# A convolution-attention and mixture-of-experts kernel: the conditions of the rare expert tiles moved behind the other conditional tiles, and filler matmuls changed in two places

## The chip, the cores and the metric

The kernel runs on one core of one Trainium2 chip. The metric is the device time of one execution in microseconds (us). A core has five engines that this text calls PE (TensorE, the matmul array), DVE (VectorE), ACT (ScalarE), POOL (GpSimd) and SP (SyncE, which only issues DMAs); each runs its own instruction stream in order, and they meet through semaphores. "PEld" is PE's weight load, "PEq" or "PEldq" is PE's sequencer, the part that fetches, branches and hands work to the array. PE's clock is granted by a throttle; the profile shows it as a share of full speed.

## The reference, cut to what matters

The input is an image of 256 channels and 48 x 48 positions, that is 2304 tokens.

```python
x = x + _L0_conv_ref(_gn(x), ...)   # layer 0: group norm, then attention over 9216 = 2304 * 4 keys
t = _to_tokens(x)
t = t + _L1_attn_ref(_ln_t(t), ...) # layer 1: attention over 64 slices
t = t + _L1_ffn_ref(_ln_t(t), ...)  # layer 1: 8 experts, each token goes to its best 2
```

The expert part is what most of the change is about:

```python
top_w, top_i = jax.lax.top_k(xf @ Wg + bg, 2)
w_dense = sum over the 2 of one_hot(top_i) * softmax(top_w)
for e in range(8):
    h = gelu(xf @ W1[e] + b1[e])                  # 256 -> 1024
    out += w_dense[:, e:e+1] * (h @ W2[e] + b2[e])  # 1024 -> 256
```

## The kernel before, in words

**Start.** `x` is loaded in five pieces and each weight matrix by its own DMA. PE begins with `busy_first(14)` (L271): 14 matmuls whose result nobody reads, which I call fillers. They write columns 256 to 511 of the PSUM tile `pgb` (L263). PE then transposes `Wq` (L272), sums DVE's statistics over groups into columns 0 to 3 of the same `pgb` (L283), runs two more fillers (L297), and sums the variances (`spread`, L293 to L295). DVE and POOL make the normalisation from that (`rsqrt`, L301), DVE normalises `x` (L311), and the projections of q, k and v follow (L320, L324, L401), in PSUM tiles `pp` of a pool of five (L248).

**Attention of layer 0.** 18 blocks of queries by 36 pairs of key blocks; PE makes scores `s`, ACT takes their exponential `p`, DVE sums, PE multiplies with the values into `av`. Layer 1's attention is spread beside it and finished in a short stage of small steps.

**Routing.** The gate's results are turned into a list of 128-row tiles, each of one expert: 2 * 2304 = 4608 rows fill at least 36 tiles (`SURE`, L38) and, rounded up for each expert, at most 43 (`NSL`, L37). How many are used, `used_i`, is known only at run time; this input uses 39. Row numbers (`slot_t`) and experts (`expert_i`) of all tiles come out of matmuls `pw`, which are followed by four small matmuls `pq` and by `busy(8, spin)` (L1202), 8 more fillers. Every matmul here is float32 and appears in the trace as two records, so 8 fillers are 16 records.

**Expert tiles.** For tile `s`, POOL gathers 128 token rows with an indirect DMA (`rows`, L1246, or four parts, `parts`, L1257), SP loads the expert's `W1` (`load_w1`, L1271), PE (`turn`, L1278) or DVE (`turn_parts`, L1287) transposes the rows into `xT`, `first` (L1297) makes 16 matmuls `ph` and 8 gelus on ACT, `second` (L1315) 8 matmuls `py` and the scaling on DVE, and `scatter` (L1335) adds the rows to DRAM with an indirect DMA of POOL. `xT`, `hid`, `ph`, `py` and `y` are taken from small rings of buffers. Which expert a tile has is read from `expert_i` into a register on each engine.

The tiles come in three kinds, and their order in the program is written out by hand:

- `FAR` to `NSL - 1`, tiles 39 to 42, the rare ones. They stand first (L1355 to L1360), as four nested conditions `used > s`; ahead of them every engine reads `used_i` into a register (L1350).
- `near`, tiles 36 to 38. Tile 36 has no condition (L1382 to L1385). Tiles 37 and 38 stand in two nested conditions (L1386 to L1391).
- tiles 0 to 35, which always run (L1395 on).

With 39 tiles in use, all conditions of tiles 37 and 38 hold, and `used > 39` fails: every engine jumps over the code of all four rare tiles at once. In that place an engine also makes up for the semaphore counts of what it skipped: the instruction EVENT_SEMAPHORE at the condition's line, which waits for the count so far and then adds; on POOL also one INC_SWDGE_SEM, after waits for earlier indirect DMAs.

The last tile's rows are added in the output stage, and a second copy of the whole program, for inputs that overflow the exponential, is skipped by a condition at the very end (L1479).

Of the kernel before, what the change touches and what calls it, by code (L numbers as in the profile page):

```python
# [9 lines left out]
FP = mybir.dt.float32  # L10
# [5 lines left out]
P = 128  # L16
# [20 lines left out]
NSL = (2 * NT - E) // P + E  # L37
SURE = 2 * NT // P  # L38
FAR = SURE + 3
# [26 lines left out]
def layers(  # L66
# [10 lines left out]
    nc = tc.nc  # L77
# [7 lines left out]
    ones = const.tile([P, P], FP, name="ones")  # L85
# [72 lines left out]
    for c, pieces in enumerate(((1152, 1152), (1152, 768, 384))):  # L158
        at = 0
# [50 lines left out]
    for h in range(H1):  # L210
        at = ((h // 2) % 2 * 2 + h // 4) * D1
# [36 lines left out]
    with proj, tc.tile_pool(name="ps_pj", bufs=5, space=PSUM) as ps_pj, tc.tile_pool(  # L248
        name="ps_g", bufs=1, space=PSUM
    ) as ps_g, tc.tile_pool(  # L250
        name="ps_w", bufs=2, space=PSUM
    ) as ps_w:
        def transposed(dst, raw):
            pw = ps_w.tile([P, 2, C], FP, name="pw", tag="pw")
            for ci in range(2):
                for co in range(2):
                    pe.transpose(
                        pw[:, ci, co * P : (co + 1) * P], raw[:, co, ci * P : (ci + 1) * P], ident
                    )
            nc.scalar.copy(dst, pw)  # L260
            return dst

        pgb = ps_g.tile([P, 512], FP, name="pgb")  # L263

        def busy_first(n):
            for _ in range(n):
                pe.matmul(
                    pgb[:, 256:512], ones, ones.unsqueeze(1).to_broadcast([P, 2, P]), start=True, stop=True
                )

        busy_first(14)  # L271
        WqT = transposed(pj.tile([P, 2, C], FP, name="WqT"), raws["Wq"])  # L272
        pg = pgb[:, 0:4].rearrange("p (a b) -> p a b", a=2)
        pb = pgb[:, 16:94]
# [33 lines left out]
        for bi, (t0, tn) in enumerate(TBLOCKS):  # L308
# [6 lines left out]
            for m in range(2):  # L315
# [11 lines left out]
                for j in range(2):  # L327
                    rows = slice(j * DK, (j + 1) * DK)
                    at = (2 * m + j) * NT + t0
# [68 lines left out]
        for i in range(NTT):  # L398
            pv = ps_pj.tile([P, 512], FP, name="pp", tag="pp")
            for c in range(2):  # L400
                nc.tensor.matmul(  # L401
                    pv[:, 0:C], xn[:, c, i * P : (i + 1) * P], WvT[:, c, :],
                    start=(c == 0), stop=(c == 1),
# [15 lines left out]
    def busy(n, bank):  # L419

        for _ in range(n):
            pe.matmul(bank[:, 0:256], ident, Wqkv_sb[:, 0, 0:256], start=True, stop=True)
# [146 lines left out]
    def attention():  # L569
# [210 lines left out]
    spin = idle.enter_context(tc.tile_pool(name="ps_spin", bufs=1, space=PSUM)).tile(  # L780
        [P, 256], FP, name="spin"
    )
# [27 lines left out]
    for c in range(2):  # L810
        pe.matmul(
            pts[:, c, :], sums_of[:, c * P : (c + 1) * P], fold.rearrange("p a s -> p (a s)"),
            start=(c == 0), stop=False,
# [9 lines left out]
    for c in range(2):  # L823
        for i in range(NTT - 2, NTT):
# [3 lines left out]
                start=False, stop=(c == 1 and i == NTT - 1),  # L828
# [22 lines left out]
    with tc.tile_pool(name="sa", bufs=1) as sa, sums_done, tc.tile_pool(  # L851
        name="ps_sc", bufs=1, space=PSUM
# [9 lines left out]
        with tc.tile_pool(name="ps_b", bufs=3, space=PSUM) as ps_b:  # L862
# [5 lines left out]
            for m in range(2):  # L868
                for c in range(2):
                    pe.matmul(  # L870
                        ph[:, m, :], W0_sb[:, c, m * P : (m + 1) * P], ts_sum[:, c * S : (c + 2) * S],
                        start=(c == 0), stop=(c == 1),
# [28 lines left out]
            for u in range(2):  # L901
                ph = ps_b.tile([P, 2, 2 * S], FP, name="ph", tag="mm")
                phs.append(ph)
                for kind in range(2):
                    j = 2 * kind + u
                    for c in range(2):
# [3 lines left out]
                            start=(c == 0), stop=(c == 1),  # L910
# [5 lines left out]
            for u in range(2):  # L916
                for r in range(4):
                    v, w = divmod(r, 2)
                    rows = slice(r * D1, (r + 1) * D1)
# [14 lines left out]
            a = sa.tile([P, 2, 2, S], FP, name="a")  # L934
# [42 lines left out]
            for w in range(2):  # L977
                pe.matmul(
                    pw, tokT[:, w].rearrange("p a s -> p (a s)"), Wout_sb[:, w, :],
                    start=(w == 0), stop=(w == 1),  # L980
# [19 lines left out]
        with tc.tile_pool(name="ps_y0", bufs=1, space=PSUM) as ps_y0:  # L1000
# [3 lines left out]
            for g, (i0, n) in enumerate(groups):  # L1004
                pys = [next(banks)[:, 0 : C + E] for _ in range(n)]
                for i in range(i0, i0 + n, 4):
                    some = range(i, min(i + 4, i0 + n))
                    for k in some:
                        u = k % 2
                        rows = slice(u * S, (u + 1) * S)  # L1010
                        pe.matmul(
                            pys[k - i0], swT[rows, k // 2, :], tw[rows, :], start=(k >= 4),
                            stop=(k < 4 or k in by_dve),
# [29 lines left out]
    used_i = route.tile([1, 1], mybir.dt.int32, name="used_i")  # L1043
# [6 lines left out]
    with gating, tc.tile_pool(name="onehot", bufs=1) as oh, tc.tile_pool(  # L1050
        name="ps_lg", bufs=1, space=PSUM
# [112 lines left out]
        for n in (3, 6, 6, 3, 6, 6, 3, 3):  # L1164
# [13 lines left out]
            for j in range(k, k + n):  # L1178
# [3 lines left out]
                    start=(j == 0), stop=(j == K - 1),  # L1182
# [16 lines left out]
                pq[:, k, :], quad[:, k, :, :].rearrange("p q s -> p (q s)"), empties, start=True, stop=True,  # L1199
            )  # L1200
        dve.tensor_scalar(part_t, pq, 4.0, quarter, ALU.mult, ALU.add)
        busy(8, spin)  # L1202

    def expert_of(s, engine):
        return nc.values_load(
# [5 lines left out]
    with tc.tile_pool(name="ps_h", bufs=1, space=PSUM) as ps_h, tc.tile_pool(  # L1211
        name="ps_y", bufs=1, space=PSUM
    ) as ps_y, tc.tile_pool(name="ps_t", bufs=1, space=PSUM) as ps_t, tc.tile_pool(
        name="ps_j", bufs=1, space=PSUM
    ) as ps_j:

        def ring(pool, n, shape, name):
            return cycle([pool.tile(shape, FP, name=f"{name}{k}") for k in range(n)])

        ring_xs, ring_w1 = ring(fp, 2, [P, C], "xs"), ring(fp, 2, [P, 2, HID], "w1")  # L1220
        ring_xT, ring_hid = ring(fp, 3, [P, 2, P], "xT"), ring(fp, 2, [P, NHC, P], "hid")
# [4 lines left out]
        near_xs = iter([fp.tile([P, C], FP, name=f"near_xs{s}") for s in range(SURE, FAR)])  # L1226
        fin = ctx.enter_context(tc.tile_pool(name="fin", bufs=1))
        far_xs, far_w1 = fin.tile([P, C], FP, name="far_xs"), fin.tile([P, 2, HID], FP, name="far_w1")
        here = fin.tile([P, NT], FP, name="here")
        held = fin.tile([P, NTT], FP, name="held")  # L1230
        obs = cycle([fin.tile([P, 2, 512], FP, name=f"ob{k}") for k in range(3)])

        issued = []

        def indirect(**kwargs):

            new = nc.gpsimd.indirect_dma_start(**kwargs)  # L1237
            if issued:
                tc.add_manual_dep(
                    new.ins, issued[-1].ins.name,  # L1240
                    mybir.DependencyInfo(mybir.DependencyClass.NoSync, mybir.DependencyReason.DATA),
                    reason="in written order",
                )
            issued.append(new)

        def rows(s, xs):  # L1246
            indirect(
                out=xs, out_offset=None, in_=tn_d[:, :],
                in_offset=bass.IndirectOffsetOnAxis(ap=slot_t[:, s : s + 1], axis=0),
                bounds_check=NT + P - 1, oob_is_err=True,  # L1250
            )
            return xs

        def in_parts(s):
            return 2 <= s < SURE and s % 4 != 1
# [15 lines left out]
        def load_w1(s, w1):  # L1271
            e = expert_of(s, mybir.EngineType.SP)
            nc.sync.dma_start(
                out=w1, in_=W1[bass.ds(e, 1)].rearrange("e (p c) f -> p (e c) f", p=P)
            )
            return w1

        def turn(xs):  # L1278

            pt = next(ring_pt)  # L1280
            for c in range(2):
                pe.transpose(pt[:, c, :], xs.rearrange("p (d c) -> p c d", c=2)[:, c], ident)
            xT = next(ring_xT)
            dve.tensor_copy(xT, pt)
            return xT

# [10 lines left out]
        def first(s, xT, w1):  # L1297

            e = expert_of(s, mybir.EngineType.Activation)
            hid = next(ring_hid)  # L1300
            for f0 in range(0, NHC, 4):
                ph = next(ring_ph)
                for f in range(f0, f0 + 4):
                    for c in range(2):
                        pe.matmul(
                            ph[:, f - f0, :], w1[:, c, f * P : (f + 1) * P], xT[:, c, :],
                            start=(c == 0), stop=(c == 1),
                        )
                for f in range(f0, f0 + 4):
                    act.activation(  # L1310
                        hid[:, f, :], ph[:, f - f0, :], AF.Gelu, bias=b1_e[:, bass.ds(e, 1), f],
                    )
            return hid

        def second(s, hid, meanwhile):  # L1315

            e = expert_of(s, mybir.EngineType.PE)
            py = next(ring_py)
            for f in range(NHC):
                pe.matmul(  # L1320
                    py, hid[:, f, :],
                    w2_sb[:, bass.ds(e, 1), f, :].rearrange("p e d -> p (e d)"),
                    start=(f == 0), stop=(f == NHC - 1),
                )
                if f == 2:
                    meanwhile()
            e = expert_of(s, mybir.EngineType.DVE)
            y = next(ring_y)
            dve.tensor_tensor(
                y, py, b2_e[:, bass.ds(e, 1), :].rearrange("p e d -> p (e d)"), ALU.add  # L1330
            )
            dve.tensor_scalar(y, y, slot_w[:, s : s + 1], None, ALU.mult)
            return y

        def scatter(s, y):  # L1335

            indirect(
                out=t_d[:, :], out_offset=bass.IndirectOffsetOnAxis(ap=slot_t[:, s : s + 1], axis=0),
                in_=y, in_offset=None, bounds_check=NT + P - 1, oob_is_err=True,
                compute_op=ALU.add,  # L1340
            )

        near = range(SURE, FAR)
        xs, w1, xT, hid = {}, {}, {}, {}
        for s in near:
            xs[s] = rows(s, next(near_xs))
        for s in range(2):
            w1[SURE + s] = load_w1(SURE + s, next(ring_w1))
            xs[s] = parts(s, next(ring_xs))
        used = nc.values_load(  # L1350
            used_i, min_val=0, max_val=NSL,
            skip_runtime_bounds_check_because="it is a sum of counts, cut at NSL",
        )

        with ExitStack() as more:  # L1355
            for s in range(FAR, NSL):
                more.enter_context(tc.If(used > s))
                issued.clear()
                far = turn(rows(s, far_xs))
                scatter(s, second(s, first(s, far, load_w1(s, far_w1)), lambda: None))  # L1360
        issued.clear()

        def turn_next(s):
            if s in xs:
                xT[s] = (turn_parts if in_parts(s) else turn)(xs.pop(s))
# [17 lines left out]
        hid[SURE] = first(SURE, xT.pop(SURE), w1.pop(SURE))  # L1383
        w1[SURE + 2] = load_w1(SURE + 2, next(ring_w1))
        scatter(SURE, second(SURE, hid.pop(SURE), more_turns))  # L1385
        with ExitStack() as more:  # L1386
            for s in near[1:]:
                more.enter_context(tc.If(used > s))
                issued.clear()
                hid[s] = first(s, xT.pop(s), w1.pop(s))  # L1390
                scatter(s, second(s, hid.pop(s), lambda: turn_next(s + 1) if s + 1 in near else None))  # L1391
        issued.clear()
        for s in range(2):
            w1[s] = load_w1(s, next(ring_w1))
# [121 lines left out]
```

## Time and profile before

| what | value |
|---|---|
| median of 4 runs | 1603.0 us (1596.97, 1600.52, 1605.49, 1609.12) |
| the profiled execution | 1598.84 us |
| its span, first to last instruction | 1597.1 us |
| mean granted PE clock | 0.997 |
| PE busy | 1566.4 us (98%) |
| DVE, ACT, POOL busy | 1037.6 (65%), 830.2 (52%), 270.5 us (17%) |
| matmuls `s` and `av` of layer 0's attention, busy | 674.8 and 675.7 us |
| matmuls `ph` and `py` of the experts, busy | 150.8 and 144.4 us |

The profile is of one execution. Its times count from the span's start. "Idle before" is the time for which an engine did nothing ahead of an instruction, and the name behind it is what released it; "issue" is time in which the engine waited for nothing that the profile shows. A PE record's duration overlaps the next one's, so sums of durations are no times; starts are compared instead.

### The profile page before, as it was taken

Reading aid. Unit: us, or ns where it says so; the run is one execution under the profiler, and the core shown is the slowest. Engines: PE = TensorE matmul, PEld = TensorE weight load, DVE = VectorE, ACT = ScalarE, POOL = GpSimd, SP = SyncE. Lnnn points to the kernel's source line nnn. Section 1 sums busy time; section 2 is a strip of 40 time slices with the busy share of each in tenths; the row PEclk is TensorE's granted clock in tenths of the full one; section 3 lists DMA queues with packets and bytes.
Section 4 is the critical chain, followed back from the end, with each engine's and each line's share of the span. In section 5 each row is a group of like instructions: output and inputs, shape, how many; then the busy total and the mean of one; then the engine's idle time right before and its main releaser. Section 6 shows DMA issues by size and latency. Waiting matters only on the chain. (4 is left out here: it accounts for less than half of the span.)

```text
span 1597.1 us, 32306 instructions
## 1 busy us (share of the span) xinstructions
PE 1566.4 (98%) x13105; PEld 781.7 (49%) x13105; DVE 1037.6 (65%) x1323; ACT 830.2 (52%) x1168; POOL 270.5 (17%) x210
## 2 busy tenths in 40 slices
PE   8999999999999999999999999999999999999998
PEld 5633343333333333333333333333335789898996
DVE  7578787787787877878878778778786711211111
ACT  2366665655665666556556556566554623322322
POOL 0001101011011010110100101101100146666571
PEclk9999999999999999999999999999999999999999
DMA  4000000000000000000000000000003846655665
GB/s 136 1 1 1 1 1 4 6 1 1 8 1 1 8 1 2 8 1 1 6 3 1 4 5 1 1 8 1 1 1 113 297 139 190 179 172 154 193 169 160
DMA packets 53071, 79.32 MB, mean 50 GB/s; under 512 B 22719, under 2 KB 43406, under 8 KB 47790
## 3 DMA queue, kind: packets, MB, share of 16 engines
q1 hardware_dynamic: 42834, 66.45, 12.6%
q0 software_dynamic: 9424, 10.10, 3.6%
q8 instruction: 108, 1.77, 0.5%
q10 hardware_dynamic: 652, 0.56, 0.1%
q14 instruction: 53, 0.43, 0.1%
HBM read 62.94 MB, written 12.32 MB: 47 GB/s over the span
## 5 line engine op out<-in xcount | busy, mean ns | idle before, releaser
L60 ACT ACTIVATE p<-s 128x1024 f32<-128x1024 f32 x648 | 663.3, 1024 | 470.4 <-PE s L60 465.8
L60 DVE TENSOR_TENSOR acc<-acc,p 128x1024 f32<-128x1024 f32 x612 | 749.5, 1225 | 243.2 <-ACT p L60 237.3
L60 PE MATMUL av<-p,v_sb 64*64 64x512 f32 x5184 | 675.7, 590 | 2.9 <-ACT p L60 1.8
L60 PE MATMUL s<-q,kk 64*64 64x512 f32 x5184 | 674.8, 589 | 0.5 <-DVE tn L60 0.5
L60 PEld LDWEIGHTS s<-q,kk 64*64 64x64 f32 x5184 | 202.1, 133 | 353.6 <-issue 181.5
L60 PEld LDWEIGHTS av<-p,v_sb 64*64 64x64 f32 x5184 | 195.6, 131 | 358.4 <-ACT p L60 201.5
L60 POOL PARTITION_ALL_REDUCE total<-both x17 | 71.2, 4187 | 1011.4 <-ACT p L60 833.5
L60 ACT ACTIVATE hid<-ph,bcol 128x128 f32<-128x128 f32 x312 | 88.8, 370 | 210.8 <-PE ph L60 118.8
L60 PE MATMUL ph<-xT,w 128*128 128x128 f32 x1248 | 150.8, 279 | 3.7 <-issue 3.3
L60 PEld LDWEIGHTS ph<-xT,w 128*128 128x128 f32 x1248 | 149.2, 195 | 7.1 <-issue 5.1
L60 PE MATMUL py<-w_sb,hid 128*128 x624 | 144.4, 380 | 2.9 <-issue 2.6
L60 PEld LDWEIGHTS py<-w_sb,hid 128*128 128x128 f32 x624 | 114.7, 190 | 18.3 <-issue 4.2
L1237 POOL DMA_INDIRECT xs<-tn_d,part_t x104 | 106.6, 1025 | 40.1 <-issue 29.3
L60 DVE TENSOR_TENSOR y<-py,b_bc 128x256 f32<-128x256 f32 x39 | 16.6, 425 | 127.1 <-PE py L60 83.4
L1237 POOL DMA_INDIRECT t_d<-y,slot_t x38 | 61.6, 1620 | 69.1 <-DVE y L60 35.6
L60 DVE STREAM_TRANSPOSE xT<-xs 128x128 f32<-128x128 f32 x52 | 13.1, 289 | 61.6 <-DMA xs<-tn_d,part_t 56.7
L60 DVE COPY xT<-pt 128x256 f32<-128x256 f32 x13 | 5.4, 424 | 54.0 <-PE pt L60 54.0
L60 DVE RECIPROCAL rinv<-rinv 128x256 f32<-128x256 f32 x17 | 29.7, 1746 | 0.0
L60 POOL TENSOR_TENSOR rstd_t<-ve,mhalf 128x2 f32<-128x2 f32 (+2 forms) x13 | 11.1, 851 | 103.4 <-DVE ve L60 96.1
L60 DVE TENSOR_TENSOR acc<-p 128x1024 f32<-128x1024 f32 x18 | 22.1, 1226 | 4.9 <-ACT p L60 3.3
L337 DVE TENSOR_SCALAR q<-pp,bcol 64x512 f32<-64x512 f32 (+1 forms) x30 | 20.8, 694 | 6.1 <-PE pp L320 5.8
L60 DVE TENSOR_REDUCE up<-av 128x512 f32<-128x1024 f32 x17 | 20.8, 1225 | 5.0 <-PE av L60 5.0
(302 smaller groups left out, 616.2 us busy)
## 6 DMA issues: line engine op xcount, KB each, us to landing
w<-in_L_ffn_W_dram SPq DMA_DIRECT2D x39, 1024.0 KB
w_sb<-in_L_ffn_W_dram SPq DMA_DIRECT2D x8, 1024.0 KB
t_sb<-turned SPq DMA_DIRECT2D x224, 8.0 KB
x_sb<-in_x_dram SPq DMA_DIRECT2D x3, 576.0 KB
xs<-tn_d,part_t POOLq DMA_INDIRECT x104
t_d<-t_sb SPq DMA_DIRECT2D x2, 768.0 KB
tn_d<-tn SPq DMA_DIRECT2D x2, 768.0 KB
t_sb<-t_d SPq DMA_DIRECT2D x3, 512.0 KB
```

The source lines that it names most:

```text
L60: return self.tc.keep_in_program_order(getattr(self.engine, name)(*args, **kwargs))
L337: nc.vector.tensor_scalar(dst, pq[rows, 0:tn], bcol[rows, B_Q + m : B_Q + m + 1], 0.125, ALU.add, ALU.mult,)
L1237: new = nc.gpsimd.indirect_dma_start(**kwargs)
```

## The change

It has four parts.

1. The fillers of the start write a PSUM tile of their own, `spun`, the first tile of the pool `pp`; `pgb` shrinks to 96 columns. The first row of fillers has 17 matmuls instead of 14. The pair of fillers at L297 stays, but in the new tile.
2. The fillers after `pq` are 6 instead of 8.
3. The read of `used_i` and the four conditions of the rare tiles move from ahead of tile 36: the read stands behind tile 36, and the rare tiles stand behind tile 38, inside the conditions of tiles 37 and 38.
4. The rare tiles take their transposed rows from a tile of their own, `far_xT`, not from the ring `xT`.

```diff
-        pgb = ps_g.tile([P, 512], FP, name="pgb")
+        pgb = ps_g.tile([P, 96], FP, name="pgb")
+        spun = ps_pj.tile([P, 512], FP, name="pp", tag="pp")
...
-                    pgb[:, 256:512], ones, ones.unsqueeze(1).to_broadcast([P, 2, P]), start=True, stop=True
+                    spun[:, 0:256], ones, ones.unsqueeze(1).to_broadcast([P, 2, P]), start=True, stop=True
...
-        busy_first(14)
+        busy_first(17)
...
-        busy(8, spin)
+        busy(6, spin)
...
+        far_xT = fin.tile([P, 2, P], FP, name="far_xT")
...
-        def turn(xs):
+        def turn(xs, xT=None):
...
-            xT = next(ring_xT)
+            xT = next(ring_xT) if xT is None else xT
...
-        used = nc.values_load(
-            used_i, min_val=0, max_val=NSL,
-            skip_runtime_bounds_check_because="it is a sum of counts, cut at NSL",
-        )
-
-        with ExitStack() as more:
-            for s in range(FAR, NSL):
-                more.enter_context(tc.If(used > s))
-                issued.clear()
-                far = turn(rows(s, far_xs))
-                scatter(s, second(s, first(s, far, load_w1(s, far_w1)), lambda: None))
-        issued.clear()
-
...
         scatter(SURE, second(SURE, hid.pop(SURE), more_turns))
+        used = nc.values_load(
+            used_i, min_val=0, max_val=NSL,
+            skip_runtime_bounds_check_because="it is a sum of counts, cut at NSL",
+        )
         with ExitStack() as more:
             for s in near[1:]:
                 more.enter_context(tc.If(used > s))
                 issued.clear()
                 hid[s] = first(s, xT.pop(s), w1.pop(s))
                 scatter(s, second(s, hid.pop(s), lambda: turn_next(s + 1) if s + 1 in near else None))
+            for s in range(FAR, NSL):
+                more.enter_context(tc.If(used > s))
+                issued.clear()
+                far = turn(rows(s, far_xs), far_xT)
+                scatter(s, second(s, first(s, far, load_w1(s, far_w1)), lambda: None))
         issued.clear()
```

In the built program PE's order around the change is: before, `pw`, `pq`, 8 fillers, read of `used_i`, jump over the rare tiles, tile 36, tile 37, tile 38, tile 0; after, `pw`, `pq`, 6 fillers, tile 36, read of `used_i`, tile 37, tile 38, jump over the rare tiles, tile 0. POOL's four part gathers for tile 2 stand ahead of tile 36's scatter in both; before, that is behind the jump, after, ahead of it. SP's load of `W1` for tile 38 stands behind the jump before and ahead of it after.

## The prediction

> **What bounds the kernel now.** I read the page first: span, busy times and clock.
>
> ```profile
> PE 1566.4 (98%) x13105; PEld 781.7 (49%) x13105; DVE 1037.6 (65%) x1323; ACT 830.2 (52%) x1168; POOL 270.5 (17%) x210
> ...
> PEclk9999999999999999999999999999999999999999
> ```
>
> PE is busy for 98% of the span at nearly full clock, and in the attention (about 45 to 1215 us) nearly without a gap. So whatever moves PE's start of the projections moves the end by as much, and so does a gap of PE among the expert tiles. The change touches three places; for each I read PE's timeline.
>
> At the start:
>
> ```profile
> 1.12 7.76 PE L60 MATMUL pgb<-ones 128*128 128x256 f32 x28 [1.12 <-DVE ones L86]
> 10.41 0.63 PE L60 MATMUL pw<-ident,Wq_raw 128*128 128x128 f32 x4 [1.53 <-DMA Wq_raw<-in_L_conv_Wq_dram]
> 11.06 0.35 PE L60 MATMUL pgb<-mv,gmat 128*128 128x2 f32 x2
> 12.12 1.13 PE L60 MATMUL pgb<-ones 128*128 128x256 f32 x4 [0.70 <-DVE mean L60]
> 13.09 0.28 PE L60 MATMUL pgb<-dm,gmat 128*128 128x2 f32 x2
> ```
>
> The second fillers (12.12) wait for DVE to have read `pgb`, only because they write the same tile; the sum over `dm`, which everything waits for, stands behind them.
>
> Between routing and experts:
>
> ```profile
> 1277.25 0.98 PE L60 MATMUL pq<-empties,quad 128*128 128x43 f32 x8
> 1278.06 3.70 PE L60 MATMUL spin<-Wqkv_sb,ident 128*128 128x256 f32 x16
> 1283.16 0.48 PE L60 MATMUL pt<-ident,near_xs 128*128 128x128 f32 x2 [1.39 <-PEq L1355]
> 1284.19 5.38 PE L60 MATMUL ph<-xT,w 128*128 128x128 f32 x32 [0.56 <-issue]
> ```
>
> PE waits 1.39 us for its own sequencer at L1355, the condition of the rare tiles. The instructions of that line, and those of the conditions of tiles 37 and 38:
>
> ```profile
> L1355 PEldq COMPARE_BRANCH x1: 4134/4134/4134, 1278.6 to 1278.6; - x1
> L1355 DVEq COMPARE_BRANCH x1: 72/72/72, 1279.0 to 1279.0; - x1
> ```
> ```profile
> L1386 PEldq COMPARE_BRANCH x3: 73/85/205, 1290.9 to 1306.2; - x3
> ```
>
> The jump over four tiles takes PE's sequencer 4.134 us, from 1278.6 to 1282.7; DVE's takes 72 ns, and a condition of PE that does not jump far 73 to 205 ns. The 16 filler records cover 3.2 us of the jump. Then the clock, in stretches of 3.41 us (columns: stretch, length, PE busy, PEld, DVE, ACT, POOL, granted clock, DMA):
>
> ```profile
> 7.51:10.92 3.41, 1.88 (x11) 1.28 (x9) 3.35 (x8) 0.00 (x0) 0.00 (x0) 1.00 0.74 238
> 10.92:14.33 3.41, 2.68 (x19) 2.21 (x17) 0.88 (x6) 0.94 (x2) 0.55 (x1) 1.00 0.81 226
> 1280.68:1284.09 3.41, 1.56 (x8) 0.92 (x6) 0.42 (x1) 0.00 (x0) 2.69 (x3) 1.00 0.42 118
> 1284.09:1287.50 3.41, 3.31 (x15) 3.34 (x16) 0.00 (x1) 0.00 (x0) 0.00 (x0) 0.50 0.14 41
> 1475.24:1478.65 3.41, 1.59 (x14) 1.49 (x13) 0.08 (x1) 0.27 (x2) 1.83 (x2) 1.00 0.12 29
> 1478.65:1482.06 3.41, 3.41 (x18) 3.41 (x18) 1.11 (x4) 1.97 (x8) 2.09 (x2) 0.50 0.79 267
> ```
>
> After a stretch in which PE was busy for 1.56 or 1.59 us the clock is halved for the next 3.41 us; after 1.88 us it is not. The price is in the timeline: tile 36's 32 `ph` records took 5.38 us, the other tiles' 3.73, so 1.65 us. The point lies at about 1.75 us busy, or 1.66 us idle.
>
> Last, where the jump goes, between tiles 38 and 0:
>
> ```profile
> 1304.78 3.62 PE L60 MATMUL py<-w_sb,hid 128*128 x16
> 1308.23 3.73 PE L60 MATMUL ph<-xT,w 128*128 128x128 f32 x32
> ```
>
> There is no gap here. The last L1386 instruction, the end of tile 38's code, is at 1306.2 on PE's sequencer: it runs 2.0 us ahead of the array's next start, 1308.23.
>
> **The change, step by step**, against the profiled execution (1598.84 us; its span is 1597.1, with 1.74 around it).
>
> *A. Fillers with a bank of their own.* The pair no longer waits for `mean`: it follows the sums at 11.06 + 0.35 = 11.41 instead of 12.12. `dm` is ready by about 12.0 (two DVE instructions of 0.35 us together from 11.65), earlier than the fillers' end. The sum over `dm` comes 13.09 - 12.12 = 0.97 after the pair's start, so at 12.38: 0.7 us sooner. Behind it every step waits for the one before (DVE `ve` 13.53, POOL 13.78, DVE `t_sb` 14.55, PE `pp` 15.15), and the transposes of `Wv`, done 0.78 us before `pp`, cover 0.7 even if their weight comes no sooner. **-0.7 us**; ends -0.7 and 0.
>
> *Three more fillers* are 6 records. 16 records in 3.70 us are 0.22 us each at full clock, so 1.3 us: 8.88 + 1.3 = 10.2, before `Wq` lands at 10.41. Idle time hides them: 0. Without that cover, at half clock, 2.6 us would end at 11.5 and delay the sums by up to 1.1. I take 0, ends 0 and +1.1.
>
> *B. Tile 36 without a jump ahead of it.* PE loses two fillers (4 records, 0.9 us) and the jump. The fillers then end at 1281.76 - 0.9 = 1280.9. Next is tile 36's gather, which POOL starts at 1277.33 (1.38 us long). The trace does not show when it landed, as PE was held by the jump. The nearest row is a later gather that DVE did wait for: start 1538.78, DVE's transpose at 1541.32, 2.54 us; with the 0.37 by which this one is longer, 1280.2. So the fillers decide, and `pt` starts at 1280.9 instead of 1283.16: **-2.25 us**; ends -2.25 and 0 (landing only just before 1283.1). PE's idle time falls from 1.39 + 0.56 to some 0.6, under 1.66, so the half clock goes too: **-1.65**; ends -1.65 and 0.
>
> *C. The jump behind tile 38.* It starts where PE's sequencer stands at 1306.2, takes 4.13 us, and 0.43 us pass from the jump's end (1282.7) to the first record, as at L1355: 1310.8 instead of 1308.23, **+2.55 us**. Nothing covers more than the 2.0 us of run-ahead counted. PE then stands idle for about 2.4 us, over 1.66; only if the edge of a stretch cuts the gap in the middle is the clock spared, in some 3 of 10 positions. **+1.65**; ends 0 and +1.65. The jump's ends: 0, if it is as short as the conditions of L1386 (0.2 us at most, under the run-ahead), and +2.55.
>
> The rest costs nothing. The read of `used_i` behind tile 36 (about half a us on a sequencer) lies under PE's run-ahead of over 2 us. On ACT, DVE and SP the jump takes under 0.1 us, in their idle time. On POOL, what stands behind the jump is the gather for tile 3; POOL must first see tile 38's scatter land (3.84 us from issue in the chain of waits: 1309.53 + 3.84 = 1313.4, and about 1 us of bookkeeping). That gather waits anyway until PE has transposed tile 1's rows, 1312.2 before, 2.55 us later now. They meet; if PE were not delayed, POOL would be late by about 2 us, and the 7 us from the gathers' landing (about 1316.55 + 2.54 = 1319.1) to PE's use (1326.1) would cover it. SP's loads are released by PE as before. `far_xT` never runs here; the ring order of the others keeps its distances.
>
> Sum: -0.7 - 2.25 - 1.65 + 2.55 + 1.65 = **-0.4 us**, so 1598.4 for this execution. The median of the four runs is 1603.0, 4.2 above the profiled one, which is among the fastest; on it the sum is **1602.6**. The jump is not saved, it is moved: from a place with 3.2 us of cover to one with 2.0.
>
> **Two rules.** The Trainium skill, "Advanced Engine Details and Errata" (Control Flow Timing), gives a compare-and-branch about 108 ns; by that C would be nearly free and the sum 1598.5. But "Runtime: NRT & Kernel Launch" (Instruction fetch mechanics) says that a taken branch to code outside the two loaded pages stops until it is fetched, and the 4134 ns agree with the latter.
>
> "TensorE: Matmul & The Clock Gate" (HAM oscillation) asks for no idle gap above about 3.4 us. By that C's gap would leave the clock alone, and the sum would be 1600.9; the row at 1280.68, with gaps of 1.39 and 0.56 only, speaks against it.
>
> **Rivals.** *R1, the jump is short or hidden behind tile 38.* For it: the 73 to 205 ns of L1386 and DVE's 72 ns. Against: the same distance cost PE 4.134 us. C falls away: 1603.0 - 0.7 - 2.25 - 1.65 = 1598.4.
>
> *R2, slower: tile 36 is held by its gather, not by the jump.* The place is PE at 1283: if the gather lands close to 1283, PE idles as before, with two fillers fewer and the half clock still there; B gives 0. Then 1603.0 - 0.7 + 2.55 + 1.65 = 1606.5. It decides from a landing later than about 1282.6, where the idle time passes 1.66. For it: POOL's first gather is longer than the rest (1.38 us against 1.01), and the chain of waits has indirect DMAs that took 3.84 us to land.
>
> *R3, the added fillers are late.* The first fillers took up to 795 ns each, the later ones 379; if that slow part lasts longer in a run, the 0.2 us of slack is gone: +1.1, 1603.7.
>
> *R4, the change of the bank does nothing* (the pair still waits): A is 0, 1603.3.
>
> **How the numbers follow.** Chances: forecast 0.45, R1 0.15, R2 0.22, R3 0.10, R4 0.08. The runs of the same kernel spread from 1597.0 to 1609.1, more than any of these cases differ from the forecast; about 0.5%, 8 us, is what a measurement can tell from no change. The range runs from R1 less 3 to R2 plus 3.5, half of the runs' spread being 6: **1595.5 to 1610**. Faster than 1595.0 has 0.12 (R1 with a favourable set of runs), slower than 1611.0 0.14 (R2 or R3 with an unfavourable one), within 0.74.
>
> **What the new profile would show.** A: the second fillers start right behind the sums, and `pp` near 14.5. B: `pt` of tile 36 under 0.3 us behind the last filler, and tile 36's 32 `ph` records in about 3.7 us. C: a COMPARE_BRANCH of some 4.1 us on PE's sequencer behind tile 38, a PE gap of 2 to 2.6 us ahead of tile 0, and tile 0's `ph` records at 5.4 us. I am wrong if that branch is short, if `pt` waits for the gather, or if PE has new gaps in the attention, where nothing is changed.

## The result, and the profile after

| | before | after |
|---|---|---|
| median | 1599.9 us (78 runs) | 1603.2 us (52 runs) |
| ratio to before, 95% interval | | 1.002 (1.0008 to 1.0032) |
| the profiled execution, its span | 1598.84, 1597.1 us | 1603.11, 1601.4 us |

The change costs 0.2%, some 3.3 us of the medians. That is under the half per cent named in the prediction, but it is on the other side of zero than the forecast, and its interval does not hold a ratio of 1. That the forecast time, 1602.6 us, comes so near to the measured 1603.2 is luck: it was reckoned from a median of four runs, 1603.0, where 78 runs have 1599.9; from that the forecast's -0.4 us would have given 1599.5.

PE's timeline of the changed kernel at the start (start, length, engine, line, operation, shapes; in brackets the idle time before and its releaser):

```profile
1.12 9.96 PE L60 MATMUL pp<-ones 128*128 128x256 f32 x34 [1.12 <-DVE ones L86]
10.92 0.63 PE L60 MATMUL pw<-ident,Wq_raw 128*128 128x128 f32 x4
...
12.57 0.28 PE L60 MATMUL pgb<-dm,gmat 128*128 128x2 f32 x2
13.44 0.26 PE L60 MATMUL pgb<-ident,brow 78*128 78x78 f32 x1 [0.59 <-DMA Wo_raw<-in_L_conv_Wo_dram]
...
15.35 0.70 PE L321 MATMUL pp<-t_sb,WqT 128*128 128x512 f32 x1 [0.78 <-DVE t_sb L312]
```

DVE's timeline of the same kernel shows who waits for the transpose of the biases (`brow`):

```profile
13.73 0.16 DVE L60 TENSOR_SCALAR ve<-pgb 128x2 f32<-128x2 f32 x1 [1.32 <-PE pgb L60]
13.81 0.23 DVE L60 COPY bcol<-pgb 128x78 f32<-128x78 f32 x1
```

The sum over `dm` comes 0.5 us sooner, yet `ve`, which needs only that sum, starts at 13.73. It reads `pgb`, and the transpose of `brow` writes another part of the same tile; that transpose waited until 13.44 for a load. (The view names the load of `Wo`; by the landings it was the last piece of the biases, in at 13.24, where before it was in at 12.31.) So `pp` starts at 15.35, 0.2 us later than before. The first fillers ended at 11.08 in this execution, later than `Wq` could have been taken. But the sums over `mv` at 11.41 follow DVE's `mv` (ready at 11.26) as closely as before (10.92 and 11.06), so the fillers are not seen to delay them.

Between routing and experts, and at the jump's new place, again PE's timeline of the changed kernel:

```profile
1277.64 2.84 PE L60 MATMUL spin<-Wqkv_sb,ident 128*128 128x256 f32 x12
1280.31 0.39 PE L60 MATMUL pt<-ident,near_xs 128*128 128x128 f32 x2
1281.22 3.84 PE L60 MATMUL ph<-xT,w 128*128 128x128 f32 x32 [0.52 <-DVE xT L60]
...
1300.23 3.62 PE L60 MATMUL py<-w_sb,hid 128*128 x16
1307.91 6.34 PE L60 MATMUL ph<-xT,w 128*128 128x128 f32 x32 [4.06 <-PEq L1379]
```

`pt` follows the fillers without a gap and tile 36 runs at full clock: this part of the gain is there. The price stands at 1307.91: 4.06 us idle and 6.34 us for tile 0's records. The instructions of the conditions' line (now L1379; min, median and max in ns):

```profile
L1379 SPq COMPARE_BRANCH  x4: 34/41/50, 1285.8 to 1286.9; - x4
L1379 PEldq COMPARE_BRANCH  x4: 65/142/5510, 1286.7 to 1307.6; - x4
L1379 DVEq COMPARE_BRANCH  x4: 43/51/67, 1289.9 to 1305.2; - x4
```

The long one is PE's jump, from 1301.69 to 1307.20: 5.510 us, where it took 4.134 before. And the clock by stretches (columns as in the prediction):

```profile
1303.00:1306.41 3.41, 0.85 (x4) 0.39 (x3) 0.78 (x2) 0.00 (x0) 1.44 (x1) 1.00 0.47 192
1306.41:1309.82 3.41, 1.91 (x9) 1.94 (x10) 0.00 (x0) 0.00 (x0) 0.13 (x1) 0.50 0.33 46
1309.82:1313.23 3.41, 3.41 (x18) 3.41 (x18) 0.00 (x0) 1.14 (x4) 0.00 (x0) 0.50 0.00 0
```

Two stretches at half clock follow the gap, not one.

What holds the jump up is in the records of single DMA packets. The profile has two "instruction" queues; the one called q8 moves code in packets of 16 KB. I take it for PE's, as in every run with a long branch of PE one of its packets starts and ends inside that branch. The packet for this jump started at 1304.79, 3.10 us after the branch; the load of `W1` for tile 1 (1 MB) moved from 1301.43 to 1305.03. Before the change the packet came 1.79 us after the branch, and no such load was moving.

### The profile page after: what moved, and what is told of

Same layout as the page of the kernel before. It is cut to its first block, busy times and chain, and to the rows that moved or that the text cites. A ratio compares the mean times of both kernels' runs of the same rounds, so it can differ in the third digit from the quotient of the medians.

```text
span 1601.4 us, 32303 instructions
## 1 busy us (share of the span) xinstructions
PE 1569.5 (98%) x13107; PEld 781.7 (49%) x13107; DVE 1037.0 (65%) x1323; ACT 829.2 (52%) x1168; POOL 270.0 (17%) x210
```

## The experiments

The theory, **J**: the move puts a jump that must fetch its code into a place with little cover, where a load delays the fetch, and the clock is halved after the gap. The rivals: **S**, the new start is what costs; **F**, the moved code disturbs what follows it, and not the jump itself. The experiments ran on chips where the kernel before takes 1583.9 us (the two parts alone, no rare code, side by side), 1584.1 us (one rare tile, both with fillers, no load) and 1584.6 us (the rest). I call the last one the third chip, and that of the profiles above the first. Times are medians, ratios are to the kernel before on the same chip.

### The two parts alone

*The start alone* (before, with part 1 of the change) and *the move alone* (after, with the old start and 8 fillers behind `pq`):

```diff
-                    pgb[:, 256:512], ones, ...
+                    spun[:, 0:256], ones, ...
-        busy_first(14)
+        busy_first(17)
```


> The kernel before with the first part of the change alone (fillers in a tile of their own, 17 instead of 14); the conditions and the 8 fillers stay as before. Theory J (the jump behind tile 38 lies bare and makes the loss): the time is that of before within 1 us, the first projection starts at 14.5 to 15.4 us, and tile 36 waits for PE's sequencer at L1355's place as before. Rival S (the fillers of the start make the loss): 2 to 3 us slower than before, with the projections later by as much.

> The changed kernel with the start of before and 8 fillers ahead of tile 36; the rare conditions stay behind tile 38. Theory J: a branch of 4 to 5.6 us on PE's sequencer behind tile 38, 7 to 7.7 us from the last py row of tile 38 to tile 0's first ph (3.45 before), tile 0's ph stage at 5.2 to 6.2 us (3.57 before); the time is that of the changed kernel plus 0 to 0.5, so 2 to 4 us over before. Rival S: the time of before, within 1 us.

Measured: the start alone 1582.22 us, 0.9991 (0.9982 to 1.0000); the move alone 1588.48 us, 1.0030 (1.0018 to 1.0042). So the start alone is some 1.4 us faster than before, a little more than J allowed. S falls, the move is the whole loss. F falls too: from tile 1 to the last `ph` it is 246.9 us in both, so nothing behind the jump is disturbed. The move's jump took 6.174 us, over the 4 to 5.6 expected, with a gap of 4.73 us behind tile 38. With the start alone, `pp` began at 14.31, since `brow` had landed and its transpose waited for nothing.

### Without the rare tiles' code

The changed kernel without the loop over the rare tiles. That code never runs for this input.

```diff
-            for s in range(FAR, NSL):
-                more.enter_context(tc.If(used > s))
-                ...
```


> The changed kernel with the code of the four rare tiles left out, which this input never runs. Theory J: no long branch, 3.5 us from the last py row of tile 38 to tile 0's first ph, tile 0's ph stage at 3.6 us, and the time is 6 to 7 us under the changed kernel, so 3 to 4 us under before. Rival S: at most 1 us under the changed kernel. Rival F (the moved code disturbs the loading of later instructions, which shows as 'issue' gaps among the tiles 0 to 35): the jump's gap goes, but the gaps after 1400 us stay and the gain is under 3 us.

Measured: 1579.72 us, 0.9975 (0.9966 to 0.9984). No branch of PE between tiles 36 and 0 takes more than 0.33 us, and `ph` of tile 0 follows `py` of tile 38 without a gap. Against the changed kernel itself (1.0020, below) code that is never run makes 0.45%, some 7 us.

### Side by side instead of nested; one rare tile instead of four

```diff
-                more.enter_context(tc.If(used > s))
-                issued.clear()
-                ...
+                with tc.If(used > s):
+                    issued.clear()
+                    ...
```


> The changed kernel with the four rare conditions side by side instead of nested, so that PE makes four jumps over one tile each. Theory J with the price set by the distance: four branches of 0.1 to 0.3 us and about 0.4 us of bookkeeping each, 2 us in all, covered by PE's run-ahead: no gap, 4 to 6 us under the changed kernel. If the price is set by the code that has to be loaded on the way, not by the distance of one jump: the branches add up to 4 us or more again, and the gap stays at 2 to 4 us.

Measured: 1588.46 us, 1.0034 (1.0021 to 1.0048), no gain. PE's branches of this kernel:

```profile
L1386 PEldq COMPARE_BRANCH x5: 176/214/3352, 1300.3 to 1307.6; - x5
```

Of four short jumps, those at 1300.31 and 1302.79 took 0.24 and 0.21 us, the one at 1303.36 took 3.352, the next 0.21. The price does not belong to a branch that is taken, nor to each tile; it falls once. PE's gap is 5.54 us even so, more than the 2 to 4 expected: the second branch comes only behind the end of `py` at 1302.45, so no work of PE is left to cover the long one.

```diff
-            for s in range(FAR, NSL):
+            for s in range(FAR, FAR + 1):
```


> The changed kernel with the code of one rare tile instead of four (tiles 40 to 42 are left out, which this input never runs), so PE's jump is a quarter as long. Theory J with the price set by the distance: a branch of 0.1 to 0.3 us and no gap, as without rare tiles. If any jump out of the straight line costs the same: 4 to 5.6 us and the gap of the changed kernel.

Measured, with the code of tiles 40 to 42 left out, which this input does not run: 1583.22 us, 0.9991 (0.9981 to 1.0002). The jump over one tile's code took 0.24 us, PE's gap was 0.68 us, and the clock stayed whole there. The Trainium skill, "Runtime: NRT & Kernel Launch" (Instruction fetch mechanics), says that a taken branch whose target lies outside the two pages loaded forces a fetch before execution can go on; these two runs, with one long branch of 3.352 us beside short ones of about 0.2, and the code packets below agree with it.

### Fillers ahead of the jump

```diff
+            busy(10, next(ring_py))
+            next(ring_py)
             for s in range(FAR, NSL):
```


> The changed kernel with 10 fillers (20 records, 4.4 us) between tile 38 and the rare conditions. Theory J, in two terms: the branch stays at 4 to 5.6 us but PE has work meanwhile, so no gap over 1 us, no half clock and tile 0's ph stage at 3.6 us instead of 6.2; the fillers cost 4.4 us where the gap was 4.1, so the time is 2 to 2.6 us under the changed kernel. If the half clock had no part in the loss: within 0.5 us of the changed kernel.

Measured: 1588.49 us, 1.0030 (1.0019 to 1.0042): no gain, against the expectation. PE's timeline of this kernel:

```profile
1302.39 4.48 PE L60 MATMUL py<-Wqkv_sb,ident 128*128 128x256 f32 x20
1307.57 0.35 PE L60 MATMUL ph<-xT,w 128*128 128x128 f32 x1 [0.69 <-PEq L1379]
1309.50 5.25 PE L60 MATMUL ph<-xT,w 128*128 128x128 f32 x31 [1.59 <-issue]
```

The fillers cover the branch, 3.731 us long and begun only at 1302.85. But they take over 4 us themselves, and after one record PE stops once more: the next 16 KB of code were fetched at 1307.24, after the jump had ended. The clock is halved all the same.

The kernel before, with 14 fillers in place of 8 ahead of its jump:

```diff
-        busy(8, spin)
+        busy(14, spin)
```


> The kernel before with 14 fillers instead of 8 ahead of the jump at tile 36. Theory J: the branch stays at 4.1 us, but 28 records last 6.1 us, over the jump's end: pt of tile 36 starts 0.9 to 1.3 us later than before, at most 0.3 us behind the last filler, and its ph stage takes 3.7 us instead of 5.2; in time within 1 us of before. It shows that the half clock belongs to the gap and not to the jump.

Measured: 1585.07 us, 1.0007 (0.9998 to 1.0016). Twelve records more, 2.6 us, shortened PE's gap from 1.39 to 0.83 us only, not to under 0.3 as expected. The branch begins 3.3 us before the fillers end, as with 8 of them (1278.56 against 1281.76, 3.2 us): PE's sequencer runs no further ahead, so more fillers move the branch back with them. Tile 36's `ph` took 3.81 us, but with the start alone, which has 8 fillers there, it did so too; so this run says nothing of the half clock.

### Without the load that stands in the way; with that load at another time

```diff
-        for s in range(2):
-            w1[s] = load_w1(s, next(ring_w1))
+        w1[0], w1[1] = load_w1(0, next(ring_w1)), next(ring_w1)
```


> The changed kernel with the load of W1 for tile 1 left out, so tile 1 is computed with weights of another expert. That load was under way (1301.4 to 1305.0) while PE's jump (1301.7 to 1307.2) took 5.51 instead of 4.13 us. If the load holds up the code that PE waits for: the branch takes 4.1 to 4.4 us and the gap is 2.5 to 3 us. If the length comes from elsewhere: 5.3 to 5.7 us as in the changed kernel.

Tile 1 then multiplies what lies in its buffer, so a part of the computation is changed. Measured: 1581.65 us in a single execution, a branch of 3.755 us, and

```profile
1298.85 3.62 PE L60 MATMUL py<-w_sb,hid 128*128 x16
1304.78 3.81 PE L60 MATMUL ph<-xT,w 128*128 128x128 f32 x32 [2.31 <-PEq L1379]
```

The gap is the 2.4 us that the forecast had, and the clock is whole. The last kernel of this row keeps the computation: tile 1's `W1` goes into the rare tiles' buffer, free all along, so that its load runs before the jump.

```diff
-        for s in range(2):
-            w1[s] = load_w1(s, next(ring_w1))
+        w1[0], w1[1] = load_w1(0, next(ring_w1)), load_w1(1, far_w1)
+        next(ring_w1)
```


> The changed kernel, with W1 of tile 1 loaded into the buffer of the rare tiles, so that its load need not wait for tile 38 to release its buffer; it then moves some 7 us sooner, before the jump, and no load moves while PE fetches the code behind it. Theory J: the branch falls from 5.5 or more to 3.6 to 4.2 us, PE's gap ahead of tile 0 to 2.2 to 2.9 us, and the time by 1.8 us, by 3.5 if the clock is not halved any more: ratio to before 1.0010 down to 0.9999. Rival L (the load only happens to stand there): branch, gap and time as in the changed kernel.

> The changed kernel itself, beside the kernel before on the same chip as the other experiments. Theory J (a bare jump behind tile 38, its code held up by the load of W1 for tile 1, and the half clock after it): the parts add up, the start alone 0.9991 and the move alone 1.003, so 1.0021, 3 to 3.5 us above before; the branch 5.5 to 6.2 us long, PE's gap ahead of tile 0 4 to 4.8 us, tile 0's ph records over 5 us. Rival I (the parts disturb each other): the ratio leaves 1.0010 to 1.0035.

Measured, on one chip: the changed kernel itself 1587.45 us, 1.0020 (1.0011 to 1.0030), as the sum of its parts; with the load elsewhere 1583.94 us, 0.9995 (0.9986 to 1.0004), 3.5 us less. PE's records of tile 0 in the two kernels, the changed one first:

```profile
1307.08 6.03 PE L60 MATMUL ph<-xT,w 128*128 128x128 f32 x32 [4.95 <-PEq L1379]
```
```profile
1306.55 5.44 PE L60 MATMUL ph<-xT,w 128*128 128x128 f32 x32 [2.43 <-PEq L1379]
```

The gap is 2.5 us shorter and the records take 0.6 us less, though the clock is halved still. The rival that the load only happens to stand there falls. PE's jump in these executions, from the sequencer's instructions and the DMA packets (us from the span's start):

| kernel | branch starts | code packet starts | branch ends | `W1` load moving |
|---|---|---|---|---|
| before (first chip) | 1278.56 | 1280.35 | 1282.69 | none |
| start alone | 1277.25 | 1279.10 | 1281.47 | none |
| after (first chip) | 1301.69 | 1304.79 | 1307.20 | 1301.43 to 1305.03 |
| after (third chip) | 1299.97 | 1303.90 | 1306.36 | 1299.67 to 1303.50 |
| move alone | 1303.82 | 1307.57 | 1309.99 | 1303.51 to 1307.44 |
| without the load | 1300.31 | 1301.65 | 1304.07 | none |
| load elsewhere | 1301.96 | 1303.29 | 1305.83 | none |
| side by side, the long branch | 1303.36 | 1304.28 | 1306.71 | 1299.98 to 1303.70 |
| fillers ahead of the jump | 1302.85 | 1304.15 | 1306.58 | 1300.09 to 1303.85 |

From the packet's start to the branch's end it is always 2.3 to 2.5 us. The packet starts 1.3 to 1.9 us after the branch where no load moves. In the changed kernel (both chips) and with the move alone the load starts 0.3 us before the branch, and the packet comes 3.1 to 3.9 us after the branch, within 0.5 us of the load's end. In the last two rows the branch begins only 3.4 and 2.8 us after the load's start, and the packet comes 0.9 and 1.3 us after the branch, 0.6 and 0.3 us behind the load's end. So what counts, by these rows, is how much of the load is left when the branch begins.

The clock after gaps of nearly one size: with the load elsewhere, and then without the load. (The edges of the stretches are reckoned from the clock's changes in the same trace, which lie whole multiples of 3.413 us apart: with the move alone, at 1232.74 and 1311.25, 23 of them.)

```profile
1303.24:1306.65 3.41, 0.98 (x6) 0.56 (x5) 0.78 (x2) 0.00 (x0) 1.40 (x1) 1.00 0.06 14
1306.65:1310.06 3.41, 3.41 (x17) 3.41 (x18) 0.00 (x0) 0.00 (x0) 0.16 (x1) 0.50 0.80 262
```
```profile
1300.13:1303.55 3.42, 2.34 (x11) 1.71 (x9) 0.78 (x2) 0.13 (x1) 0.00 (x0) 1.00 0.34 43
1303.55:1306.96 3.41, 2.18 (x19) 2.21 (x20) 0.00 (x0) 0.05 (x1) 1.56 (x1) 1.00 0.35 45
1306.96:1310.37 3.41, 3.41 (x29) 3.30 (x28) 0.84 (x3) 2.35 (x8) 0.91 (x1) 1.00 0.24 39
```

A gap of 2.43 us inside one stretch halves the next; one of 2.31 us that the edge at 1303.55 cuts in two halves none. The Trainium skill, "TensorE: Matmul & The Clock Gate" (HAM oscillation), would let both pass, as they are under its 3.4 us; the first of these rows is against it.

### The start again: the biases out of the way of `ve`

The start alone, with the transposed biases in the fillers' tile:

```diff
-        pb = pgb[:, 16:94]
+        pb = spun[:, 256:334]
```


> The kernel before with the new start alone, and the transposed biases put into the fillers' tile, so that DVE's first step of the normalisation (ve) no longer reads a tile that the transpose of the biases writes. Theory T (the wait for the biases' load ate the gain of the start): ve comes right after the sum over dm, 0.4 to 0.8 us sooner than with the new start alone, the projections start at 13.6 to 14.3 us instead of 14.3 to 15.35, and the time is 0.4 to 0.8 us below that of the new start alone, ratio about 0.9987. Rival (the weights' transposes or POOL set the start of the projections anyway): no difference from the new start alone, ratio 0.9991.

Measured: 1582.91 us, 0.9990 (0.9981 to 0.9999), no different from the start alone. Theory T falls, and its rival holds. PE's and DVE's timelines of this kernel:

```profile
13.17 0.26 PE L60 MATMUL pp<-ident,brow 78*128 78x78 f32 x1 [0.74 <-DMA Wo_raw<-in_L_conv_Wo_dram]
13.27 0.60 PE L60 MATMUL pw<-ident,Wk_raw 128*128 128x128 f32 x4
13.71 0.60 PE L60 MATMUL pw<-ident,Wv_raw 128*128 128x128 f32 x4
14.22 1.55 PE L321 MATMUL pp<-t_sb,WqT 128*128 128x512 f32 x3
```
```profile
12.47 0.16 DVE L60 TENSOR_SCALAR ve<-pgb 128x2 f32<-128x2 f32 x1 [0.48 <-PE pgb L60]
13.47 0.24 DVE L60 COPY bcol<-pp 128x78 f32<-128x78 f32 x1 [0.84 <-PE pp L60]
```

`ve` is free at 12.47, as wanted. But the load of the biases holds PE itself, ahead of the transposes of `Wk` and `Wv`, and these now end right where `pp` starts; and `bcol` holds DVE ahead of `t_sb`.

### A version that beats both

The jump stays ahead of tile 36, and its cover is arranged: `pq`, which only later gathers need, goes behind tile 36's transposes, and one row of 9 fillers stands between `pw` and the jump. The start is that of the last experiment. `quad`, which `pq` reads, moves to a pool that lasts as long as needed.

```diff
-        busy(4, spin)
+        busy(9, spin)
...
-        pq = ps_lg.tile([P, 4, NSL], FP, name="pq")
-        for k in range(4):
-            pe.matmul(pq[:, k, :], ...)
-        dve.tensor_scalar(part_t, pq, 4.0, quarter, ALU.mult, ALU.add)
-        busy(8, spin)
...
         turn_next(SURE)
+        pq = next(ring_ph)[:, :, 0:NSL]
+        for k in range(4):
+            pe.matmul(pq[:, k, :], ...)
+        dve.tensor_scalar(part_t, pq, 4.0, quarter, ALU.mult, ALU.add)
         hid[SURE] = first(SURE, xT.pop(SURE), w1.pop(SURE))
```


> The kernel before with the new start, the biases in the fillers' tile, and the jump ahead of tile 36 as in the kernel before, but sooner: the four matmuls pq with part_t stand behind the transposes of tile 36, and the fillers (9 in one row instead of 4 and 8) ahead of the jump. Theory J: a jump costs what its cover lacks. The branch starts some 1.5 to 2 us sooner relative to pw, the fillers cover most of it, tile 36's pt follows 5.0 to 6.0 us after the last pw instead of 7.7, pq fills part of PE's wait for xT, and the time is 1 to 2.5 us below that of the new start with its biases moved: ratio 0.997 to 0.998, below both kernels. Rival K (the branch waits for PE's own earlier work, so it begins no sooner than the fillers end): no gain, and pq adds 0.4 to 1 us, ratio 0.999 or above.

Measured: 1579.19 us, 0.9969 (0.9957 to 0.9981), 3.7 us under the same start without this edit and 8.3 under the changed kernel. PE's timeline:

```profile
1274.92 4.09 PE L60 MATMUL spin<-Wqkv_sb,ident 128*128 128x256 f32 x18
1280.03 0.48 PE L60 MATMUL pt<-ident,near_xs 128*128 128x128 f32 x2 [1.02 <-DMA near_xs<-tn_d,slot_t]
1280.35 0.99 PE L60 MATMUL ph<-empties,quad 128*128 128x43 f32 x8
1281.16 3.82 PE L60 MATMUL ph<-xT,w 128*128 128x128 f32 x32
```

The branch takes 3.773 us, from 1275.64 to 1279.41, and is no longer what PE waits for: `pt` now waits for tile 36's gather, which POOL started at 1276.76. From `pw`'s end to `pt` it is 4.95 us against 7.63 in the same start without this edit. That is 2.7 of the 3.7 us; where the rest comes from these two profiles do not show. Rival K falls.

## Why the prediction was wrong, by its steps

| step | forecast | first chip, after less before | other chips |
|---|---|---|---|
| A, start of `pp` | -0.7 | +0.2 | -0.84 (14.31 less 15.15) |
| B, `pq` to `pt` | -2.25 | -2.43 | -2.55 |
| B, half clock at tile 36 | -1.65 | -1.55 | 0 |
| C, gap ahead of tile 0 | +2.55 | +4.23 | +5.11 |
| C, half clock at tile 0 | +1.65 | +2.61 | +2.30 |
| sum | -0.4 | +3.1 | +4.0 |

(Half clock: what the 32 `ph` records took. The last column is the third chip's profile of the changed kernel less that of the start alone, and for A the start alone less the move alone. Each profile is of one execution; by the times the sum is +3.3 us on the first chip and, by the ratio 1.0020, +3.2 on the third.)

**B held.** The fillers decide, `pt` follows them, and R2 does not happen. It was closer than I made it: in the last experiment the gather needed 3.27 us from POOL's start to `pt`, not the 2.91 reckoned, which puts its landing in the changed kernel at 1276.90 + 3.27 = 1280.17, hardly before `pt` at 1280.31. The half clock that goes was the state of one execution: with the start alone PE's gaps at this place were 1.52 and 0.56 us, an edge at 1281.14 divided the first (2.69 and 2.05 us busy in the stretches on either side), and the clock stayed whole.

**C failed in its size, and with it the sign.** "It starts where PE's sequencer stands at 1306.2, takes 4.13 us": where the branch stands was right, 2.2 us ahead of the end of `py`; its duration was taken as that of the distance jumped. It is that of a fetch, and the fetch waits for the DMA engines. At the new place `load_w1` of tile 1 waits for tile 38's last `ph`, which frees its buffer, and PE's sequencer reaches the jump 0.3 us after that load starts. So the two met in all three executions profiled (the changed kernel on two chips, the move alone): 5.5 to 6.4 us. Without the load the forecast's term stands (branch 3.755, gap 2.31). I had followed SP's queue for waits, and had not asked what its load would do to a fetch.

**C's half clock** was one stretch in the forecast; the changed kernel's gaps of 4.06 and 4.95 us left two, +2.6 and +2.3 us instead of +1.65. The length of the gap alone does not decide it: with the move alone 4.73 us left one (+1.70).

**A's step "Behind it every step waits for the one before" was incomplete.** `ve` waits for the whole tile `pgb`, so also for the transpose of `brow` and the load behind it. Where that load has landed (12.39 in the changed kernel on the third chip) the chain is as reckoned: `pp` at 14.31, the forecast's 14.45. In the profiled execution it had not. R3's late fillers were there too (their end at 11.08 instead of about 10.2), but not its cost: the sums behind them were held by DVE's `mv`. The late biases do not show in the medians: the start alone is 1.4 us faster, though its interval just reaches a ratio of 1.

R1 and R4 do not happen. In the first chip's two profiles three differences in code that is the same are left over: 0.6 us less between `pp` and `pq` after than before, 2.9 us more in the rest of the tile stage, and 0.9 us less behind it. In that rest PE is idle for 7.04 us before and 8.83 after; 5.4 and 7.3 us of it are put down to "issue", in gaps of up to 1.1 us that are at other places in either execution; in the changed kernel on the third chip that stretch has none over 0.3 us, and it lasts 246.9 us there and in nearly all experiments, where the first chip's profiles have 259.2 and 262.1. What makes them on the first chip stays open.

## What to carry over

Price a jump over much code as a DMA of code: ask when the sequencer reaches it, what load is released at that moment, and which of the array's queued work lasts until the fetch is done. A conditional block that is never run is cheapest where no load moves and PE's next work waits for something else anyway; fillers help only up to the sequencer's run-ahead. And a reader of one part of a tile waits for writers of its other parts, with all that they wait for.

## What was not expected of the hardware

- A code packet of 16 KB waits for a 1 MB load that began shortly before: 3.1 to 3.9 us from branch to packet instead of 0.9 to 1.9. Its own transfer takes about 1 us.
- The fetch may come in two steps: in the run with fillers the branch was over, one matmul ran, and PE stopped for another 1.59 us around a second packet. That is one execution; without the load a second packet followed too (1304.72), and PE ran on. Why it stopped here is open.
- PE's sequencer runs 3.2 to 4.0 us ahead over a row of fillers, whether 16, 18, 20 or 28 records stand there.
- Busy time alone does not decide the clock. With the move alone, a stretch with 1.56 us busy (1304.42 to 1307.84) left the next at full clock, and 0.55 us in that one halved the one after; the prediction's rows had 1.56 and 1.59 halved. In the changed kernel 1.91 us busy at half clock kept it halved. So the prediction's point of about 1.75 us busy does not hold; where it lies, if there is one, is open.
